# Layer 1 of a graph attention network: one row of a tile moved from TensorE to the other engines, with a pair of rows added on GpSimd

## The chip, the cores and the metric

One core of a Trainium2 chip runs the kernel. The metric is the device time of one execution in microseconds. Of the kernel before there are ten runs, and one more execution was taken by the profiler. The engines are called TensorE (PE; its weight loads PEld), VectorE (DVE), ScalarE (ACT), GpSimd (POOL) and SyncE (SP, here only a DMA queue).

## The reference

Two layers of graph attention over 10,000 nodes and 170,000 edges (80,000 random pairs in both directions, and a loop at every node), then a norm. Cut to what matters:

```python
def gat_conv(x, edge_index, W, a_src, a_dst, bias, heads, out_ch, concat):
    xl = (x @ W).reshape(n, heads, out_ch)
    alpha_src = jnp.einsum('nhc,hc->nh', xl, a_src)
    alpha_dst = jnp.einsum('nhc,hc->nh', xl, a_dst)
    e = leaky_relu(alpha_src[src] + alpha_dst[dst], 0.2)
    e = exp(e - segment_max(e, dst)[dst])
    alpha = e / (segment_sum(e, dst)[dst] + 1e-16)
    msg = xl[src] * alpha[:, :, None]
    return segment_sum(msg, dst) + bias           # concat or mean over heads

h  = gat_conv(x, edge_index, W1, ..., 4 heads, 256)   # layer 1
h1 = relu(layer_norm(h, g1, be1)) + (x @ Wr1 + br1)
h  = gat_conv(h1, edge_index, W2, ..., 1 head, 768)   # layer 2
h  = layer_norm(h, g2, be2) + (h1 @ Wr2 + br2)
out = layernorm(x + h)
```

## The kernel before

The kernel runs in three phases. The first computes the table of all nodes, `table1`: a row holds 1024 features (4 heads of 256) and its attention numbers. Beside it, it sorts the nodes by their number of edges into 79 tiles of 128 nodes. Layer 1 then takes one tile after the other, and layer 2 does the same on `table2`, with another division of the work.

The nodes of a tile lie in the 128 partitions. A tile has as many *rows* (`SLOTS[t]`) as its nodes have edges at most: row k holds, for each of the 128 nodes, the table row of its k-th neighbour, 1033 numbers. The rows are fetched by an indirect DMA that GpSimd issues (`gather`, L426) into a ring of 29 rows (`RING1`); a row's place is fetched anew when the row has been used (`ring.fetch` at the end of each k). Tiles of 14 to 17 rows are 29 of the 79: 6 of 14, 8 of 15, 7 of 16 and 8 of 17. They stand in two groups, tiles 7 to 21 and 58 to 71. None of them is cut into parts (`cuts_of` does that from 22 rows on).

For a tile of n rows the work in layer 1 is:

- The softmax of its weights `e` (`logits` and `normalised`, L489 to L514): VectorE, with one exponent on ScalarE (L497). It is the first step of the generator `weights_of(t)`.
- A weighted sum over its rows, in `acc` (PSUM). Each row is done in one of three ways. The first `on_pe(t)` rows go to TensorE: ScalarE builds four diagonal matrices from the weights (L725), TensorE multiplies them with the row (L731). Of the others, every `SHARE`-th, counted from the first, VectorE multiplies and adds by itself (`weigh`, L531, four instructions, one for each head). The rest are *shared*: ScalarE multiplies the row in place (`multiply`, L520, four instructions), VectorE adds it to `acc` (L527, one instruction).
- A norm of the sum (L542 to L558, with two small steps on ScalarE, L546 and L547), the residual (L856), a transposition, the products with `wr1` (L173) and with `w2` (L879) on TensorE, and the stores.

The kernel sets the order of each engine's instructions by hand (`manual_schedule`), so an instruction that waits holds up all that is behind it on its engine. In the loop over k, ScalarE is kept `LEAD` = 3 rows ahead (`multiplied(k + 1 + LEAD)`). The next tile's softmax is put between the last rows: `weights_of(t + 1)` takes its first step at k = n - 3 and its second, with the diagonals and TensorE's rows, at k = n - 2. The third step, with the rows beyond two for TensorE, comes at the start of the next tile, just after VectorE's statistics and the two steps L546 and L547. After row `first + 2`, GpSimd also issues the gather of the next tile's `x` rows (`xt`), and after `first` and `first + 1` the two halves of `hT` are copied by ScalarE (L698).

The rule for TensorE's rows is `min(max(SLOTS[t] // 2 - 5, 1), ON_PE1, SLOTS[t])`: 2 rows of 14 or 15, 3 of 16 or 17.

Of the kernel before, what the change touches and what calls it, by code (L numbers as in the profile page):

```python
# [48 lines left out]
LEAD = 3  # L49
DIAGONALS = 5  # L50
ON_PE2 = 512
SHARE = 4
ON_PE1 = 4
PARTED2 = 26
PARTED = 22


def chunk_counts(n_edges):
# [23 lines left out]
def gnn_kernel(ctx, tc, x, x_cols, src, dst, src_col, dst_col, W1, a_src1, a_dst1, b1, g1, be1, Wr1, br1,  # L82
               W2, a_src2, a_dst2, b2, g2, be2, Wr2, br2, out, n_edges):
    nc = tc.nc
# [3 lines left out]
    C1, C2 = H1 * DH1, H2 * DH2  # L88
# [3 lines left out]
    NT = -(-N // P)  # L92
# [4 lines left out]
    SLOTS = CAPS  # L97
# [3 lines left out]
    FIRST, TOTAL = [0] * NT, 0  # L101
# [414 lines left out]
    def multiply(row, e, dh):  # L516

        for h in range(e.shape[1]):
            s = slice(h * dh, (h + 1) * dh)
            nc.scalar.activation(row[:, s], row[:, s], AF.Copy, scale=e[:, h:h + 1])  # L520
# [122 lines left out]
    SLOTS, FIRST = [SLOTS[t] for t in TURNS], [FIRST[t] for t in TURNS]  # L643
# [4 lines left out]
    def begin_layer2(mem):  # L648


        rest = mem.shape[1]

        def at_end(n):
            nonlocal rest
            rest -= n
            return mem[:, rest:rest + n]

        firsts = [(at_end(C1), at_end(D0)) for _ in range(min(2, NT))]
        for t, (hT, xt) in enumerate(firsts):
            nc.sync.dma_start(hT, h1_d[turns[t]])  # L660
            nc.sync.dma_start(xt, x_d[turns[t]])
        wr2 = wr1.rearrange("p k n -> p (k n)")[:, :K1 * C2].rearrange("p (k n) -> p k n", n=C2)
        load(wr2, Wr2)
        br, ones = at_end(C2), at_end(P)
        yield
        nc.vector.memset(ones, 1.0)
        nc.vector.tensor_scalar(br, wr2[:, 0, :], br1_c[:, 0:1], None, op0=OP.mult)
        for k in range(1, K1):
            nc.vector.scalar_tensor_tensor(br, wr2[:, k, :], br1_c[:, k:k + 1], br, op0=OP.mult, op1=OP.add)
        yield wr2, firsts, br, ones, rest  # L670
# [4 lines left out]
    def ordered_layer1(mem):  # L675
        nc.scalar.add_instruction(mybir.InstLoadActFuncSet(name=nc.get_next_instruction_name(), act_func_set_id=6, engine=nc.scalar.engine))
        with tc.tile_pool(name="b1", bufs=1) as pool, tc.tile_pool(name="small1", bufs=2) as small, \
# [3 lines left out]
            ring = Ring(table1, RING1, {}, [mem.rearrange("p (k n) -> p k n", n=R1)])  # L681
# [30 lines left out]
            def on_pe(t):  # L712


                return min(max(SLOTS[t] // 2 - 5, 1), ON_PE1, SLOTS[t])

            def later_on_pe(t):

                return min(max((SLOTS[t] - 20) // 2, 1), ON_PE1)
# [61 lines left out]
            def cuts_of(t):  # L781

                n = SLOTS[t]
                groups = 1 if n < PARTED else -(-2 * n // ring.size)
                size = 8 if groups == 2 else (n - 5) // groups
                return [0] + [n - size * g for g in range(groups - 1, -1, -1)]

            def by_vector(t, k):
                lo = max(c for c in cuts_of(t)[:-1] if c <= k)
                return k - lo >= (later_on_pe(t) if lo else on_pe(t))  # L790

            def shared(t, k):
                return by_vector(t, k) and (k - on_pe(t)) % SHARE > 0

            last = None
            full = None
            ready = []
            ahead = iter(())
# [17 lines left out]
            for t in range(NT + 1):  # L816
                live, events = t < NT, []
                n = SLOTS[t] if live else 0
                first = done = on_pe(t) if live else 0
                cuts = cuts_of(t) if live else []  # L820
                if live and not ready:
                    ahead = weights_of(t)
                    ready += itertools.islice(ahead, 2)

                def row_of(k):
                    lo = max(c for c in es if c <= k)
                    return es[lo][0][:, k - lo], es[lo][1] if k == lo else None

                def multiplied(upto):
                    nonlocal done  # L830
                    while done < min(upto, n):
                        if shared(t, done):
                            multiply(ring.slot(FIRST[t] + done), row_of(done)[0], DH1)
                        done += 1

                if not live:
                    begin = begin_layer2(mem)
                    next(begin)
                later = iter(())
                if live:  # L840
                    es, acc = ready
                    es, later = dict(es), ahead
                if last:
                    r_before, means = last
                    stats = deviation(small, pieces(means[:, :C1], BANK))
                next(later, None)
                if full is not None:
                    store(t - 2)
                moves = []
                if live and t:  # L850
                    xT, moves = from_x(t)
                multiplied(first + 2)
                if last:
                    h = pool.tile([P, C1], F32, name="h")
                    scaled(h, [means[:, :C1]], stats, g1_b, be1_b)
                    nc.vector.scalar_tensor_tensor(h, h, 0.0, r_before[:, :C1], op0=OP.max, op1=OP.add)  # L856
                if not live:
                    begun = next(begin)
                for move in moves:
                    move()  # L860
                multiplied(first + LEAD)
                if last:
                    hT = pool.tile([P, K1, P], F32, name="hT")
                    events = [(first + j, move) for j, move in enumerate(halves(hT, h))]
                def by_wr1():
                    nonlocal r
                    if live and t:
                        r = product(xT, wr1, C1, ps_r)

                by_wr1()  # L870

                def to_layer2():
                    nonlocal full
                    nc.sync.dma_start(h1_d[t - 1], hT.rearrange("p k n -> p (k n)"))
                    full = []
                    for c in range(0, R2, BANK):
                        q = ps_half.tile([P, BANK], F32, name="half")[:, :min(BANK, R2 - c)]
                        for j in range(K1):
                            nc.tensor.matmul(q, hT[:, j, :], w2[:, j, c:c + q.shape[1]],  # L879
                                             start=(j == 0), stop=(j == K1 - 1))  # L880
                        full.append((c, q))

                if last:
                    events.append((cuts[1] - 2 * LEAD if len(cuts) > 2 else first + 2, to_layer2))

                def next_x():
                    nonlocal xt
                    xt = fetch_x(t + 1)

                if t and t + 1 < NT:  # L890
                    events.append((first + 2, next_x))
                events.sort(key=lambda event: event[0])

                def due(k):
                    while events and events[0][0] <= k:
                        events.pop(0)[1]()

                ready = []
                ahead = iter(())
                if live and t + 1 < NT:  # L900
                    ahead = weights_of(t + 1)
                for k in range(n):
                    if k + 2 * LEAD + 2 in cuts[1:-1]:
                        next(later)
                    if k + 2 * LEAD in cuts[1:-1]:
                        lo, es_lo = next(later)
                        es[lo] = es_lo
                    multiplied(k + 1 + LEAD)
                    if n - LEAD <= k < n - LEAD + 2:
                        ready += itertools.islice(ahead, 1)  # L910
                    if k + 2 in cuts[1:-1]:
                        next(later)
                    weights, fade = row_of(k)
                    if fade is not None:
                        for h in range(H1):
                            s = slice(h * DH1, (h + 1) * DH1)
                            nc.vector.scalar_tensor_tensor(acc[:, s], acc[:, s], fade[:, h:h + 1], ring.slot(FIRST[t] + k)[:, s],
                                                           op0=OP.mult, op1=OP.add)
                    if by_vector(t, k):
                        weigh(acc, ring.slot(FIRST[t] + k), weights, DH1, shared=shared(t, k))  # L920
                    ring.fetch(FIRST[t] + k + 1 + ring.size)
                    due(k)
                due(DEGREES)
                ready += itertools.islice(ahead, max(2 - len(ready), 0))
                last = None
                if live:
                    last = r, acc
# [459 lines left out]
```

## Time and profile before

| what | us |
|---|---|
| median of ten runs | 5180.73 (5172.89 to 5183.17) |
| the profiled execution | 5187.01 |
| its span, first to last instruction | 5185.2 |
| granted TensorE clock, mean | 0.964 |

Over the whole span TensorE is busy for 4766.1 us (92%), VectorE for 4281.9 (83%), GpSimd for 3301.4 (64%), ScalarE for 2818.0 (54%). The stages differ, though. Busy time in each, with the two stretches that hold the tiles of 14 to 17 rows apart:

| stretch, us from the start | what | long | PE | DVE | ACT | POOL | clock | DMA | GB/s |
|---|---|---|---|---|---|---|---|---|---|
| 0 to 907 | the table, the sorting | 907.00 | 857.65 | 482.01 | 357.95 | 436.39 | 0.98 | 0.40 | 111 |
| 1082.8 to 1500.5 | layer 1, tiles 7 to 21 | 417.70 | 405.05 | 387.22 | 317.43 | 264.13 | 1.00 | 0.96 | 353 |
| 1500.5 to 2776.8 | layer 1, longer tiles | 1276.30 | 1152.18 | 1148.73 | 1024.89 | 845.53 | 0.96 | 0.96 | 355 |
| 2776.8 to 3165.4 | layer 1, tiles 58 to 71 | 388.60 | 371.55 | 360.96 | 294.06 | 246.85 | 1.00 | 0.97 | 353 |
| 3333 to 5185 | layer 2 | 1852.00 | 1663.74 | 1597.84 | 590.26 | 1340.88 | 0.94 | 0.95 | 351 |

"DMA" is the mean busy share of the 16 DMA engines. A line of a timeline in this document reads: start, duration, engine, line of the kernel, operation, output<-input, shapes, how many instructions were merged, and in brackets how long the engine was idle ahead of them and what ended it.

### The profile page before, as it was taken

To read this page: it belongs to the slowest core of one execution; us is meant where nothing else is said; L and a number is where in the kernel's file an instruction comes from. 1 tells how busy PE (TensorE), PEld (TensorE's weight loads), DVE (VectorE), ACT (ScalarE), POOL (GpSimd) and SP (SyncE) were. 2 spreads that over 40 slices of the span, in tenths; PEclk is the share of its full clock that TensorE was granted. 3 is DMA by queue.
4 is the path that set the end of the run, shared out by engine and by line. 5 is a ranking of instruction groups with operands and counts; after the bars stand their busy time and mean duration, and the time that the engine had idled before them with its cause. 6 is when DMAs were issued, how large, how long until landed. Compare 5 with 4: busy or idle time off the path is not lost. (4 is left out here: it accounts for less than half of the span.)

```text
span 5185.2 us, 60341 instructions
## 1 busy us (share of the span) xinstructions
PE 4766.1 (92%) x15307; PEld 2864.5 (55%) x15307; DVE 4281.9 (83%) x7678; ACT 2818.0 (54%) x8248; POOL 3301.4 (64%) x3429
## 2 busy tenths in 40 slices
PE   8999998899999988788999999999999999888875
PEld 3444443455555555555555555556666666665654
DVE  4785243899999888889999999789999888888887
ACT  3443443677778887887888777433333333333232
POOL 2445455656666666666666665277777777777774
PEclk9999999899999999999999999999999999999987
DMA  4333533999999999899999999599999999999996
GB/s 160 124 102 85 90 93 126 348 336 352 358 371 370 364 350 353 297 348 351 370 371 367 359 346 337 187 384 357 367 378 376 371 365 364 362 358 357 353 350 219
DMA packets 474312, 1591.43 MB, mean 307 GB/s; under 512 B 118327, under 2 KB 122487, under 8 KB 473958
## 3 DMA queue, kind: packets, MB, share of 16 engines
q0 software_dynamic: 322384, 1286.62, 67.6%
q1 hardware_dynamic: 149520, 297.43, 16.7%
q10 hardware_dynamic: 2054, 3.42, 0.2%
q8 instruction: 129, 2.11, 0.2%
q14 instruction: 225, 1.84, 0.1%
HBM read 1431.80 MB, written 177.29 MB: 310 GB/s over the span
## 5 line engine op out<-in xcount | busy, mean ns | idle before, releaser
L426 POOL DMA_INDIRECT ring<-table,slots x2675 | 2661.6, 995 | 1281.3 <-issue 311.0
L531 DVE SCALAR_TENSOR_TENSOR acc<-ring,e,acc 128x256 f32<-128x256 f32 (+1 forms) x2546 | 1586.5, 623 | 122.2 <-PE acc L731 47.0
L520 ACT ACTIVATE ring<-ring,e 128x256 f32<-128x256 f32 x3232 | 1320.6, 508 | 0.0
L527 DVE TENSOR_TENSOR acc<-acc,ring 128x1024 f32<-128x1024 f32 x808 | 994.9, 1231 | 72.7 <-ACT ring L520 5.1
L173 PE MATMUL big<-w,xT 128*128 128x512 f32 x1896 | 825.6, 597 | 23.6 <-DMA w<-in_W_dram 10.2
L879 PE MATMUL half<-w,hT 128*128 128x512 f32 (+1 forms) x2528 | 830.4, 486 | 0.0
L173 PE MATMUL big<-wr,xT 128*128 128x512 f32 x1896 | 829.8, 594 | 0.2 <-ACT xT L698 0.2
L1033 PE MATMUL big<-wr,w 128*128 128x512 f32 (+1 forms) x2464 | 819.7, 486 | 0.0
L988 PE MATMUL big<-ring,diagonals 128*128 128x256 f32 x2754 | 679.8, 409 | 135.3 <-ACT diagonals L987 113.5
L988 PEld LDWEIGHTS big<-ring,diagonals 128*128 128x128 f32 x2754 | 559.2, 206 | 253.5 <-ACT diagonals L987 154.0
L879 PEld LDWEIGHTS half<-w,hT 128*128 128x128 f32 x2528 | 477.7, 189 | 367.7 <-issue 309.3
L1033 PEld LDWEIGHTS big<-wr,w 128*128 128x128 f32 x2464 | 468.1, 190 | 326.6 <-issue 294.8
L731 PE MATMUL acc<-ring,diagonals 128*128 128x256 f32 x2056 | 511.7, 406 | 127.7 <-ACT diagonals L725 120.0
L173 PEld LDWEIGHTS big<-w,xT 128*128 128x128 f32 x1896 | 361.7, 191 | 483.1 <-issue 462.7
L173 PEld LDWEIGHTS big<-wr,xT 128*128 128x128 f32 x1896 | 355.4, 191 | 418.0 <-issue 417.4
L731 PEld LDWEIGHTS acc<-ring,diagonals 128*128 128x128 f32 x2056 | 413.1, 204 | 222.5 <-ACT diagonals L725 148.7
L987 ACT ACTIVATE diagonals<-ident,e 128x128 f32<-128x128 f32 x1377 | 411.4, 387 | 154.3 <-DVE e L511 124.5
L546 ACT ACTIVATE sd<-mv,eps 128x1 f32<-128x1 f32 x237 | 69.5, 293 | 751.4 <-DVE mv L544 751.2
L630 DVE TENSOR_TENSOR scr<-big,ad_b 128x1024 f32<-128x1024 f32 x79 | 96.7, 1224 | 377.0 <-ACT row L627 377.0
L725 ACT ACTIVATE diagonals<-ident,e 128x128 f32<-128x128 f32 x1028 | 315.2, 388 | 166.6 <-DVE e L511 145.3
L635 POOL TENSOR_TENSOR row<-row,none 128x1024 f32<-128x1024 f32 x79 | 187.3, 2371 | 262.8 <-ACT row L627 262.3
L497 ACT ACTIVATE e<-e 128x32 f32<-128x32 f32 (+26 forms) x174 | 41.1, 236 | 552.5 <-DVE e L496 526.5
(185 smaller groups left out, 3651.2 us busy)
## 6 DMA issues: line engine op xcount, KB each, us to landing
ring<-table,slots POOLq DMA_INDIRECT x2675, 7.0
table<-row SPq DMA_DIRECT2D x79, 516.0 KB, 3.5
h_d<-hT SPq DMA_DIRECT2D x79, 512.0 KB, 6.8
w<-h_d SPq DMA_DIRECT2D x77, 512.0 KB, 8.4
table<-row SPq DMA_DIRECT2D x79, 385.0 KB, 6.1
ring<-table SPq DMA_DIRECT2D x79, 385.0 KB, 6.4
xT<-in_x_cols_dram SPq DMA_DIRECT2D x79, 384.0 KB, 4.5
x_d<-xt SPq DMA_DIRECT2D x79, 384.0 KB, 6.7
```

Of the source, the lines that this page charges most:

```text
L173: nc.tensor.matmul(p[:, c:e], aT[:, j, :], w[:, j, c:e], start=(j == 0), stop=(j == k - 1))
L426: nc.gpsimd.indirect_dma_start(out=to, out_offset=None, in_=table, in_offset=bass.IndirectOffsetOnAxis(ap=index, axis=0), **more)
L520: nc.scalar.activation(row[:, s], row[:, s], AF.Copy, scale=e[:, h:h + 1])
L527: nc.vector.tensor_add(acc[:, :c], acc[:, :c], row[:, :c])
L531: nc.vector.scalar_tensor_tensor(acc[:, s], row[:, s], e[:, h:h + 1], (acc if first is None else first)[:, s], op0=OP.mult, op1=OP.add)
L635: nc.gpsimd.tensor_add(row[:, :C1], row[:, :C1], b1_b)
L725: nc.scalar.activation(diagonals[:, k * H1 + i, :], ident, AF.Copy, scale=e[:, k, i:i + 1])
L731: nc.tensor.matmul(acc[:, c:d], diagonals[:, k * H1 + i, :], ring.slot(q + k)[:, c:d], start=(k == 0 and c % BANK == 0), stop=(k == m - 1 ...
L879: nc.tensor.matmul(q, hT[:, j, :], w2[:, j, c:c + q.shape[1]], start=(j == 0), stop=(j == K1 - 1))
L987: nc.scalar.activation(diagonals[:, (k - lo) % G, :], ident, AF.Copy, scale=e[:, k - lo, :])
L988: nc.tensor.matmul(to, diagonals[:, (k - lo) % G, :], ring.slot(at + k)[:, ON_PE2:C2], start=False, stop=(k == n - 1), skip_group_check=True)
L1033: nc.tensor.matmul(r[:, c:d], hT[:, j, :], wr2[:, j, c:d], start=False, stop=(j == K1 - 1 and d < C2), skip_group_check=True)
```

## The change

In tiles of 14 to 17 rows of layer 1, and there alone:

- TensorE takes one row fewer: 1 of 14 or 15, 2 of 16 or 17.
- Of the other rows VectorE does every fifth by itself, not every fourth. ScalarE multiplies the rest.
- GpSimd adds the eighth of these rows (number 7, counted from 0) to the ninth (number 8), after ScalarE has multiplied both; VectorE leaves out number 7 and adds number 8 alone.
- Where the next tile too has 14 to 17 rows, the first two steps of `weights_of(t + 1)` stand at k = n - 4 and n - 3, and ahead of `multiplied(k + 1 + LEAD)`, not behind it.

```diff
+PAIRED = 14, 17
...
             def on_pe(t):
-                return min(max(SLOTS[t] // 2 - 5, 1), ON_PE1, SLOTS[t])
+                return min(max(SLOTS[t] // 2 - 5 - paired(t), 1), ON_PE1, SLOTS[t])
+
+            def paired(t):
+
+                return t < NT and PAIRED[0] <= SLOTS[t] <= PAIRED[1]
...
             def shared(t, k):
-                return by_vector(t, k) and (k - on_pe(t)) % SHARE > 0
+                return by_vector(t, k) and (k - on_pe(t)) % (SHARE + paired(t)) > 0
...
+                    early = paired(t) and paired(t + 1)
+                    if early and n - LEAD - 1 <= k < n - LEAD + 1:
+                        ready += itertools.islice(ahead, 1)
                     multiplied(k + 1 + LEAD)
-                    if n - LEAD <= k < n - LEAD + 2:
+                    if not early and n - LEAD <= k < n - LEAD + 2:
                         ready += itertools.islice(ahead, 1)
+                    if paired(t) and k == first + 5:
+                        one, two = (ring.slot(FIRST[t] + first + j)[:, :C1] for j in (7, 8))
+                        nc.gpsimd.tensor_add(two, two, one)
...
-                    if by_vector(t, k):
+                    if by_vector(t, k) and not (paired(t) and k == first + 7):
                         weigh(acc, ring.slot(FIRST[t] + k), weights, DH1, shared=shared(t, k))
```

## The prediction

> **What bounds the kernel now.** I began with the busy time by stage. The tiles of 14 to 17 rows run in two stretches of layer 1, from 1082.8 to 1500.5 us (15 tiles) and from 2776.8 to 3165.4 us (14 tiles), 806 us of the span together. Then I took one tile of 16 rows and one of 14, each from one end of the norm (L856) to the next.
>
> ```profile
> core 0: us, PE busy (x) PEld busy (x) DVE busy (x) ACT busy (x) POOL busy (x), PEclk, DMA share, GB/s
> 1300.13:1327.78 27.65, 27.19 (x94) 16.26 (x93) 25.76 (x40) 21.29 (x58) 17.26 (x20) 1.00 0.99 367
> 3113.74:3139.17 25.43, 24.97 (x83) 14.31 (x83) 23.75 (x37) 19.94 (x54) 15.13 (x17) 1.00 0.96 350
> ```
>
> Two engines are full at once. TensorE is idle for 0.46 us of 27.65. VectorE is idle for 1.89 us, but in 40 instructions: 47 ns each, the step from one to the next and no wait. ScalarE has 6.4 us to spare and GpSimd 10.4. So relief of TensorE alone brings no more than VectorE gives up too, and a new wait on VectorE lengthens the tile by its whole size. When such a wait could arise is told by the order of time inside the tile, so next I read the timelines of ScalarE, VectorE and GpSimd in that 16-row tile.
>
> ```profile
> 1297.28 0.29 ACT L546 ACTIVATE sd<-mv,eps 128x1 f32<-128x1 f32 x1 [2.31 <-DVE mv L544]
> 1297.61 0.20 ACT L547 ACTIVATE sd<-sd 128x1 f32<-128x1 f32 x1
> 1297.72 1.26 ACT L725 ACTIVATE diagonals<-ident,e 128x128 f32<-128x128 f32 x4
> 1298.88 0.83 ACT L805 COPY row<-half 128x512 f32<-128x512 f32 x2
> 1299.62 1.71 ACT L520 ACTIVATE ring<-ring,e 128x256 f32<-128x256 f32 x4
> 1301.48 0.86 ACT L698 COPY xT<-half 128x512 f32<-128x512 f32 x2 [0.15 <-PE half L697]
> 1302.22 3.31 ACT L520 ACTIVATE ring<-ring,e 128x256 f32<-128x256 f32 x8
> 1305.43 1.05 ACT L698 COPY hT<-half 128x512 f32<-128x512 f32 x2
> 1306.37 9.69 ACT L520 ACTIVATE ring<-ring,e 128x256 f32<-128x256 f32 x24
> ```
>
> ScalarE waits for VectorE's mean and variance (L546) and then works without a gap through the multiplied rows. It is not ahead by a whole ring; it starts each tile from that wait.
>
> ```profile
> 1301.27 2.06 DVE L531 SCALAR_TENSOR_TENSOR acc<-ring,e,acc 128x256 f32<-128x256 f32 x4
> 1303.44 3.91 DVE L527 TENSOR_TENSOR acc<-acc,ring 128x1024 f32<-128x1024 f32 x3
> 1307.38 2.06 DVE L531 SCALAR_TENSOR_TENSOR acc<-ring,e,acc 128x256 f32<-128x256 f32 x4
> 1309.55 3.91 DVE L527 TENSOR_TENSOR acc<-acc,ring 128x1024 f32<-128x1024 f32 x3
> ```
>
> VectorE takes the rows that TensorE doesn't: one row on its own (L531, 4 instructions), three that ScalarE multiplied (L527, one add each), and so on. I number them v0, v1, ... A row on its own takes 2.17 us to the next start (1301.27 to 1303.44), a shared one 1.31 (3.94/3). Four products of ScalarE take 1.60 (1302.22 to 1305.43 is two rows). ScalarE finishes v7 at 1306.37 + 3 x 1.60 + 0.10 = 1311.27, and VectorE adds it at 1309.55 + 2 x 1.337 = 1312.22: 0.95 us of lead, the smallest in the tile.
>
> ```profile
> 1307.57 0.97 POOL L426 DMA_INDIRECT xt<-in_x_dram,order x1 [0.30 <-DVE acc L527]
> 1308.85 0.99 POOL L426 DMA_INDIRECT ring<-table,slots  x1 [0.30 <-issue]
> 1310.14 0.99 POOL L426 DMA_INDIRECT ring<-table,slots  x1 [0.30 <-issue]
> 1311.44 0.99 POOL L426 DMA_INDIRECT ring<-table,slots  x1 [0.31 <-issue]
> ```
>
> GpSimd issues one gather per row, 1.30 us apart, and just here is behind the rows.
>
> **The change, part by part.** Counts for the 6, 8, 7 and 8 tiles of 14, 15, 16 and 17 rows come from the code; zero of the clock below is VectorE's start on v0 (1301.27).
>
> *TensorE* loses one row in each of 29 tiles: 8 of the 24 matmuls that take 5.35 us in this tile (its timeline, L731), 1.78 us. That frees TensorE to 1.8 + 0.46 us of slack; on the path it is worth only VectorE's waits for it, 2.7 us over all 29 tiles (idle time before L531, released by L731: 2.1 us in the first stretch, 0.6 in the second).
>
> *VectorE.* 15 to 17 rows: own rows fall from 4 to 3, adds rise by one (15 and 16 rows: 9 to 10; 17: 10 to 11), since the pair counts as one. 4 x 0.525 = 2.10 less 1.31 is 0.8 us saved, on the path, x23 = 18.4 us. 14 rows: own rows 3 and adds 9 both before and after, nothing saved.
>
> *ScalarE* multiplies two rows more (14 rows: one), 3.2 us, and builds four diagonals fewer, 1.17 (1297.72 to 1298.88). Its 21.29 us become some 23.3, below the tile. In tiles of 16 and 17 rows the four that go are those between L547 and L805 (14 and 15 rows have none there now), so it comes to v1 earlier. The total is covered; the order is not.
>
> *The pair.* GpSimd adds v7 into v8, and VectorE skips v7 and waits for GpSimd before it adds v8. The add has the shape of phase one's L635, 128x1024 fp32 from SBUF: 79 of them took 2.347 to 2.398 us, median 2.37, while VectorE was busy beside them, and those that waited for ScalarE began 0.08 us after its copy. Now the clock. ScalarE from L546 at -3.99: L546 and L547 0.44, L805 0.74, the xT copies 0.74, the hT copies 0.94, and the seven rows v1, v2, v3, v4, v6, v7, v8 at 1.60 = 11.2; sum 14.06, with 0.1 for the last one's end: v8 is multiplied at 10.2. GpSimd has issued v4's gather by 1311.13, that is 9.86, so it is just free; the add runs 10.25 to 12.62, and VectorE can start v8 at 12.7. VectorE comes there at 2.17 + 4 x 1.31 + 2.17 + 1.31 = 10.9. It stands for **1.8 us**, and behind it in its queue are v9 and up, the next tile's softmax, the statistics, L546 and so the next tile's ScalarE start: the wait comes back in each tile and nothing catches it up. It doesn't depend on the row count, because v0 to v8 are alike in all 29.
>
> Bounds of the wait: were the add as quick as VectorE's own (L527, 1.23), it would be 0.7. If ScalarE gains nothing from the diagonals that go (the xT copies still wait for TensorE as now), v8 is 1.3 us later and the wait is 3.1. A full gather (0.99) ahead of the add would make it 2.8. I take 1.8, as the shape is L635's and TensorE's slack ends the xT wait.
>
> The Trainium skill, "GPSIMD Engine Reference", section 2.1 "Instruction dispatch", says that the first call of freshly loaded code on GpSimd costs some 6 us without an instruction in the profile. By that, should gathers and adds displace one another, the 29 adds would cost 29 x 6 = 174 us more; the trace speaks against it, as phase one's adds stand between gathers and of the 262.8 us idle before all 79 of them 262.3 are ScalarE's copy.
>
> *GpSimd's queue.* Queued behind the add is v5's gather, issued at about 12.8 instead of 10.2, 2.6 us late; at 1.30 us each the gathers catch up near the tile's end (v13's at about 24.5, two of TensorE's rows by 27, the next tile's v0 at 31). They fetch rows for the tile after next. The last row that the next softmax needs is asked for at k = S(t)+S(t+1)-30, at most 4, so at v2, ahead of the add; it lands 7.3 us after its issue (median of the DMA view in the first stretch), near 12.4, and the softmax starts after 15. Cost nothing; without that cover each us late is one more wait for VectorE (L489).
>
> *Softmax one row sooner*: rows are counted from the tile's start and VectorE begins one row sooner, so it stands ahead of the same v row as now (v10 for 16 rows). ScalarE's exponent is put ahead of the last multiplied row, needed about 4 us later. Nothing.
>
> **Sum.** 29 x 1.8 = 52.2; less 18.4; less 2.7: +31 us. That is against the profiled execution (span 5185.2, 5187.0 with what lies around it, 6.3 above the median of the ten runs); put on the median 5180.7 it gives **5212 us**. Break-even is a wait of (18.4 + 2.7)/29 = 0.73 us a tile.
>
> **Rivals.**
> *TensorE is the bound and the add is in time* (faster). For it: TensorE's 0.46 us of idle time, and all of the pair lies on engines with room. It decides where the add begins before 8.5 (10.9 less 2.4), so ScalarE would have to finish v8 1.7 us sooner than its own cadence gives; it starts from VectorE's L544 and has no idle time to lose. Then -18.4 - 2.7: 5160.
> *The wait only eats the saving* (no change): a wait of 0.4 to 1.1 us, as by the lower bound. 5180. It needs a faster add or a faster ScalarE than any row shows.
> *GpSimd falls behind for good* (slower still): if the 2.6 us are not caught up and the softmax waits for its rows, that is up to 29 x 2.6 = 75 us more, 5287. Against it: 10.4 us of GpSimd's idle time in the tile, and its 0.3 us steps show it keeps up once rows take 1.31 or more. The loading of code above would be slower by more, 5386.
>
> **How the numbers follow.** Forecast 0.80 (waits of 1.2 to 3.1: 5194 to 5250), slower still 0.07 (the loading of code 0.01 of it), no change 0.07, faster 0.06. A measurement tells 0.2% here, 10 us, from no change: slower 0.87, same 0.07, faster 0.06. Range 5186 to 5250: it leaves out most of the small cases on each side.
>
> **What would show it.** Right: in the tiles of 14 to 17 rows VectorE idle ahead of one L527-type add per tile (v8), released by GpSimd, 29 times, 1.8 us each; the new GpSimd add at 2.37 us, starting within 0.1 us of ScalarE's eighth-row products; 16-row tiles of some 28.7 us, 14-row tiles of 27.2; TensorE idle 2 us and more in each; other stages unchanged. Wrong: no such wait, or tiles shorter than now (TensorE or VectorE was the only bound), or VectorE waiting for DMA ahead of the softmax (GpSimd's lateness), or TensorE still without idle time.

## The result and the profile after

The changed kernel takes 5210.93 us in the median of 8 runs (5203.46 to 5218.51). The kernel before takes 5180.15 us (median of 28 runs, those beside the changed kernel included). The ratio is 1.006, 95% interval 1.0052 to 1.0069: 0.6% slower, 31 us. The forecast was 5212.

The profiled execution of the changed kernel has a span of 5204.7 us, 19.5 more than before's. Its two stretches with the tiles of 14 to 17 rows now run from 1082.5 to 1515.7 and from 2786.3 to 3190.0 us: 433.2 and 403.7 us, together 836.9 against 806.2 (taken from one L856, now L861, to the other). That is +30.7, the whole of the difference between the medians. The longer tiles between them took 1270.6 us instead of 1276.3 and layer 2 some 5 us less in that one execution, where no instruction was changed; why, is open. From here on the sum of the two stretches is used beside the ratio.

Line numbers after the change: the products of ScalarE are L521, VectorE's add L528, its own rows L532, the softmax's first instruction L490, TensorE's rows L736, the copies of xT and hT L699. GpSimd's new add is L921.

The same windows as before, one tile of 16 rows and one of 14:

```profile
core 0: us, PE busy (x) PEld busy (x) DVE busy (x) ACT busy (x) POOL busy (x), PEclk, DMA share, GB/s
1336.83:1365.55 28.72, 26.05 (x86) 15.02 (x86) 25.19 (x38) 23.20 (x63) 20.25 (x23) 1.00 0.97 352
3135.43:3162.60 27.17, 24.32 (x78) 13.50 (x78) 23.74 (x36) 20.44 (x55) 18.54 (x19) 1.00 0.94 335
```

The tile of 16 rows grew from 27.65 to 28.72 us, the one of 14 rows from 25.43 to 27.17, though TensorE is busy for 1.1 and 0.65 us less and VectorE for 0.6 us less and the same. TensorE's idle time rose from 0.46 to 2.67 us, and VectorE's from 1.89 to 3.53 in the tile of 16. Both engines that were full now stand, so a wait has come in. The timelines of VectorE and GpSimd in that 16-row tile:

```profile
1345.42 2.06 DVE L532 SCALAR_TENSOR_TENSOR acc<-ring,e,acc 128x256 f32<-128x256 f32 x4
1347.59 1.23 DVE L528 TENSOR_TENSOR acc<-acc,ring 128x1024 f32<-128x1024 f32 x1
1350.61 2.57 DVE L528 TENSOR_TENSOR acc<-acc,ring 128x1024 f32<-128x1024 f32 x2 [1.79 <-POOL ring L921]
```
```profile
1346.84 0.99 POOL L427 DMA_INDIRECT ring<-table,slots  x1 [0.30 <-issue]
...
1348.21 2.36 POOL L921 TENSOR_TENSOR ring<-ring 128x1024 f32<-128x1024 f32 x1 [0.39 <-ACT ring L521]
1350.72 1.00 POOL L427 DMA_INDIRECT ring<-table,slots  x1
```

VectorE has added v6 by 1348.82 and begins v8 at 1350.61: 1.79 us idle, and the releaser is GpSimd's add, which itself waited for ScalarE until 1348.21. VectorE's start on v0 is 1337.97 in this tile, so the add begins at 10.24 on the prediction's clock (worked out there as 10.25) and VectorE goes on at 12.64 (12.7). All 29 adds together, from the profile's view of line 921: the three numbers behind x29 are the shortest, the median and the longest in ns; behind a releaser or a waiting line stand the total us and the number of times.

```profile
L921 POOL TENSOR_TENSOR ring<-ring x29: 2353/2362/2377, 1093.9 to 3174.0; 128x1024 f32<-128x1024 f32 x29
...
ACT ring L521: 9.7, 25
who waited for it (us, times):
DVE acc L528: 53.2, 29
```

53.2 us in 29 tiles is 1.83 us each.

One thing changed that the forecast had not named, the granted clock of TensorE. Over the two stretches it was 1.00 before and is 0.96 after:

```profile
1082.50:1515.70 433.20, 393.65 (x1245) 225.66 (x1246) 378.81 (x564) 342.80 (x899) 298.13 (x312) 0.96 0.94 339
2786.30:3190.00 403.70, 363.16 (x1140) 206.20 (x1140) 353.64 (x528) 317.16 (x827) 275.28 (x290) 0.96 0.95 339
```

In 14 places the trace shows a granted clock of 0.5 for 3.4 or 6.8 us, 61 us together; a product of L174 took 1061 ns there and 592 elsewhere (medians). TensorE's busy time in the stretches fell by 19.8 us (776.6 to 756.8), not by 29 x 1.78 = 51.6; half of the 61 us is about the difference. It cost no time here, because TensorE was idle for at least 1.37 us in every one of the 29 tiles.

### The profile page after: what moved, and what is told of

Its sections match the earlier page's. It is cut to its first block, busy times and chain, and to the rows that moved or that the text cites. A ratio compares the mean times of both kernels' runs of the same rounds, so it can differ in the third digit from the quotient of the medians.

```text
span 5204.7 us, 59923 instructions
## 1 busy us (share of the span) xinstructions
PE 4739.4 (91%) x15075; PEld 2831.5 (54%) x15075; DVE 4264.8 (82%) x7609; ACT 2865.8 (55%) x8340; POOL 3355.5 (64%) x3458
## 5 line engine op out<-in xcount | busy, mean ns | idle before, releaser
L532 DVE SCALAR_TENSOR_TENSOR acc<-ring,e,acc 128x512 f32<-128x512 f32 (+1 forms) x2454 | 1541.3, 628 | 114.1 <-PE acc L736 42.9
L521 ACT ACTIVATE ring<-ring,e 128x256 f32<-128x256 f32 x3440 | 1409.8, 509 | 0.0
L528 DVE TENSOR_TENSOR acc<-acc,ring 128x1024 f32<-128x1024 f32 x831 | 1023.4, 1232 | 124.3 <-POOL ring L921 53.2
L174 PE MATMUL big<-w,xT 128*128 128x512 f32 x1896 | 825.4, 597 | 23.8 <-DMA w<-in_W_dram 10.5
L174 PE MATMUL big<-wr,xT 128*128 128x512 f32 x1896 | 845.0, 603 | 0.2 <-ACT xT L699 0.2
L174 PEld LDWEIGHTS big<-w,xT 128*128 128x128 f32 x1896 | 361.7, 191 | 483.3 <-issue 462.8
L174 PEld LDWEIGHTS big<-wr,xT 128*128 128x128 f32 x1896 | 362.5, 195 | 427.3 <-issue 426.7
L736 PE MATMUL acc<-ring,diagonals 128*128 128x256 f32 x1824 | 458.3, 408 | 121.5 <-ACT diagonals L730 109.1
L998 ACT ACTIVATE diagonals<-ident,e 128x128 f32<-128x128 f32 x1377 | 412.3, 387 | 162.5 <-DVE e L512 128.1
L736 PEld LDWEIGHTS acc<-ring,diagonals 128*128 128x128 f32 x1824 | 368.5, 205 | 207.7 <-ACT diagonals L730 134.2
L730 ACT ACTIVATE diagonals<-ident,e 128x128 f32<-128x128 f32 x912 | 279.9, 388 | 136.8 <-DVE e L512 116.3
```

The lines of the kernel that those rows point to most:

```text
L174: nc.tensor.matmul(p[:, c:e], aT[:, j, :], w[:, j, c:e], start=(j == 0), stop=(j == k - 1))
L528: nc.vector.tensor_add(acc[:, :c], acc[:, :c], row[:, :c])
L532: nc.vector.scalar_tensor_tensor(acc[:, s], row[:, s], e[:, h:h + 1], (acc if first is None else first)[:, s], op0=OP.mult, op1=OP.add)
L730: nc.scalar.activation(diagonals[:, k * H1 + i, :], ident, AF.Copy, scale=e[:, k, i:i + 1])
L736: nc.tensor.matmul(acc[:, c:d], diagonals[:, k * H1 + i, :], ring.slot(q + k)[:, c:d], start=(k == 0 and c % BANK == 0), stop=(k == m - 1 ...
L998: nc.scalar.activation(diagonals[:, (k - lo) % G, :], ident, AF.Copy, scale=e[:, k - lo, :])
```

## The experiments

Ten more runs were profiled in three groups, each group with the kernel before timed on the same chip. On the chip of the first two groups layer 2 took longer, whatever the kernel: the profile of b0_before has a span of 5518.7 us, with 301 GB/s in layer 2 where the first profile has 351, but 806.8 us in the two stretches. So each ratio is against the kernel before on the same chip, and the stretches can be compared across all.

| run | ratio (95%) | two stretches, us | tiles of 14, 15, 16, 17 rows, median us |
|---|---|---|---|
| before, first profile | | 806.2 | 25.89, 27.70, 27.80, 29.18 |
| b0_before | | 806.8 | 25.89, 27.71, 27.80, 29.18 |
| changed, first profile | 1.006 (1.0052 to 1.0069) | 836.9 | 27.23, 28.72, 28.75, 30.07 |
| a0_after | 1.0063 (1.0048 to 1.0078) | 839.1 | 27.46, 28.74, 28.81, 30.10 |
| e1_no_pair | 1.003 (1.0014 to 1.0047) | 823.2 | 26.90, 28.27, 28.30, 29.67 |
| e2_pair_9_11 | 1.0057 (1.0041 to 1.0072) | 835.5 | 28.26, 29.05, 29.17, 28.58 |
| e3_tensor_row_only | 1.0069 (1.005 to 1.0087) | 846.8 | 27.64, 29.09, 29.14, 30.50 |
| e4_share5_only | 0.9988 (0.9978 to 0.9998) | 798.8 | 26.08, 26.93, 27.90, 28.42 |
| e5_no_early | 1.0045 (1.0029 to 1.0061) | 837.5 | 27.41, 28.70, 28.76, 30.02 |
| e6_own_row_ahead | 0.9974 (0.9964 to 0.9985) | 795.4 | 25.50, 26.87, 28.30, 28.27 |
| e7_pair_keep_tensor | 1.0033 (1.0019 to 1.0048) | 825.3 | 26.64, 27.42, 28.64, 29.92 |
| e8_two_rows_ahead | 0.996 (0.9947 to 0.9974) | 785.8 | 25.56, 26.84, 26.92, 28.27 |

**e1_no_pair.** The changed kernel without the pair.

```diff
-                    if paired(t) and k == first + 5:
-                        one, two = (ring.slot(FIRST[t] + first + j)[:, :C1] for j in (7, 8))
-                        nc.gpsimd.tensor_add(two, two, one)
...
-                    if by_vector(t, k) and not (paired(t) and k == first + 7):
+                    if by_vector(t, k):
```

> The changed kernel without GpSimd's add: VectorE adds the eighth row by itself. Theory (VectorE stands 1.8 us a tile for the pair, which spares it one add of 1.31): per tile of 15 to 17 rows one own row less (2.10) and two adds more (2.62) than before, +0.5 x 23; per tile of 14 rows one add more, +1.3 x 6; less the 2.7 us of waits for TensorE: +17 us, 5197, so 14 us faster than the changed kernel though an engine's help is taken away. Rival (the loss comes from ScalarE's added rows or the gathers, not from the pair): the 29 adds of 1.31 come on top, 5211 + 38 = 5249.

The stretches are 823.2 us: +17.0 over before, as the theory has it, and 13.7 less than with the pair. VectorE took back 29 adds and the kernel became faster. The pair costs more than it spares.

**e3_tensor_row_only** and **e4_share5_only.** The other two edits, each alone, without the pair and with the softmax where it was. The lines are shown against the changed kernel.

```diff
 e3:
-                return by_vector(t, k) and (k - on_pe(t)) % (SHARE + paired(t)) > 0
+                return by_vector(t, k) and (k - on_pe(t)) % SHARE > 0
 e4:
-                return min(max(SLOTS[t] // 2 - 5 - paired(t), 1), ON_PE1, SLOTS[t])
+                return min(max(SLOTS[t] // 2 - 5, 1), ON_PE1, SLOTS[t])
```

> Only TensorE's row is taken away; VectorE does every fourth row by itself as before, no pair, softmax where it was. Theory (VectorE is full as well): one own row more in 14-row tiles (2.1 x 6), one add more in the others (1.31 x 23), less 2.7: +40, 5220. Rival (TensorE is what bounds these tiles): 1.78 us less in each of 29, 5128.

> Only every fifth row instead of every fourth is VectorE's own; TensorE keeps its row, no pair. Theory (TensorE and VectorE are both full): VectorE has 0.8 us less in tiles of 15 to 17 rows, but TensorE lets through only what it has idle: some 0.8 in the eight tiles of 15 rows and 0.75 in the eight of 17, nothing in 14 and 16: about -12, 5168. Rival (VectorE alone bounds): -18 and more, 5160. Rival (TensorE alone bounds): no change, 5180.

e3: +40.6 us in the stretches, where TensorE as the only bound would have given -52. e4: -7.4 us against before, and in the medians by tile size what two full engines let through: 15 rows -0.77 us, 17 rows -0.76, while 14 and 16 rows, where TensorE was idle for only 0.46 us in most tiles, gained nothing (two of the seven tiles of 16 rows did get shorter, by 0.8 and 0.9 us). The total is 5 us short of the -12 expected; two tiles of this execution (30.0 and 30.6 us, of 17 and 16 rows) hold most of that, and why they are long is open. Either edit alone is held by the other engine.

**e2_pair_9_11.** The pair is moved to where ScalarE is further ahead: row 9 is added into row 11.

```diff
-                    if paired(t) and k == first + 5:
-                        one, two = (ring.slot(FIRST[t] + first + j)[:, :C1] for j in (7, 8))
+                    if paired(t) and k == first + 8:
+                        one, two = (ring.slot(FIRST[t] + first + j)[:, :C1] for j in (9, 11))
...
-                    if by_vector(t, k) and not (paired(t) and k == first + 7):
+                    if by_vector(t, k) and not (paired(t) and k == first + 9):
```

> The changed kernel with another pair: GpSimd adds row 9 into row 11, issued three rows later. Theory (the place of the pair costs, not GpSimd's work): ScalarE has row 11 multiplied at 13.4 on the tile's clock, the add runs to 15.9, VectorE comes to row 11 at 16.4 after the softmax and row 10: no wait, VectorE's saving of 0.8 x 23 and 2.7 us stays, 5159, faster than before by 0.4%. Rival (the add costs GpSimd's queue or the gathers, wherever it stands): 5200 or more, with VectorE waiting for DMA or for GpSimd.

The wait for the add was gone (0.2 us in all) and the lost time was still there: 835.5 us. The expectation failed. The rival's size came true, but not the waits that it named: VectorE waited for no DMA in these tiles. It is *busy* where it had waited. The softmax's first instruction in a tile of 16 rows before, then the timelines of VectorE and GpSimd in the same tile of this run:

```profile
1289.00 0.29 DVE L489 TENSOR_TENSOR e<-ring 128x24 f32<-128x24 f32 x2
```
```profile
1305.76 3.91 DVE L528 TENSOR_TENSOR acc<-acc,ring 128x1024 f32<-128x1024 f32 x3
1309.58 2.41 DVE L490 TENSOR_TENSOR e<-ring 128x24 f32<-128x24 f32 x2
1312.02 0.23 DVE L191 SCALAR_TENSOR_TENSOR e<-e 128x64 f32<-128x64 f32 x1
```
```profile
1308.90 0.99 POOL L427 DMA_INDIRECT ring<-table,slots  x1 [0.30 <-issue]
1309.91 2.01 POOL L921 TENSOR_TENSOR ring<-ring 128x1024 f32<-128x1024 f32 x1
```

L490 adds two small operands, both in SBUF; before (as L489) it took 0.29 us in this tile, as two instructions, and 0.22 where it is one. Here it takes 2.41 and ends just behind GpSimd's add (1311.92). In each of the 21 tiles of 14 to 16 rows one small softmax instruction with two operands in SBUF was drawn out in this way, until 0.03 to 0.09 us behind the add's end: L490 in ten tiles, L191 in nine, L497 in two, 48 us together. In tiles of 17 rows the softmax stands behind row 10: there VectorE's own row 10 (L532, one operand in PSUM and one in SBUF) ran beside the add at its usual 0.49 us each, and L490 met only the end of the add in six of the eight (it took 0.3 to 0.75 us; 1.55 in the first of these tiles, and in one the two did not meet). Those are the fast tiles: 28.58 us, 0.6 less than before. The Trainium skill, "GPSIMD Engine Reference", states that GpSimd's interfaces to SBUF are shared with VectorE, with contention against VectorE instructions that have two SBUF inputs (sections 1 "Specifications" and 8 "Key points"). The trace agrees and adds the size: such an instruction ends only when the add is over, which made 0.2 to 0.3 us into as much as 2.7. The add itself lasts 2.0 us; the two longest of these instructions (2.66 and 2.68 us) began 0.6 us ahead of its recorded start, and what held them there is open.

**e5_no_early.** The softmax back at k = n - 3.

```diff
-                    early = paired(t) and paired(t + 1)
+                    early = False
```

> The changed kernel with the softmax at its old place, k = n - 3 and behind the multiplication. Theory (the softmax's place costs and brings nothing): as the changed kernel, 0.6% slower than before, the two stretches 837 us together. Rival (it hides TensorE's start): 1 us or more a tile on top, 866 us.

837.5 us: the place of the softmax brings and costs nothing, with the wait there. (The ratio is lower than the changed kernel's 1.006. On that chip 31 us of 5520 are 0.56%, which lies inside the interval.)

**e7_pair_keep_tensor.** TensorE keeps its row, so in tiles of 16 and 17 rows ScalarE still builds four diagonals ahead of the multiplied rows. The edit is that of e4 in `on_pe` with `early = False`, the pair left in.

> The changed kernel with TensorE's row kept as before (2 of 14 and 15 rows, 3 of 16 and 17) and the softmax at its old place. Theory (ScalarE's order sets the wait): in tiles of 16 and 17 rows the four diagonals stand ahead of the multiplied rows again, 1.17 us, so VectorE waits 3.0 us there and 1.8 in tiles of 14 and 15; with its work 1.31 less in 14-row tiles and 2.1 in the others that is 6 x 0.5 - 8 x 0.3 + 15 x 0.9 = +14 us, 820 us in the two stretches. Rival (GpSimd's queue sets the wait): 1.8 in all of them, -4 us, 802.

The waits for the add, with total us, times and the longest:

```profile
DVE acc L528 <- POOL ring L921: 74.2, 29, 3.3
```

By tile the median wait is 2.98 us with 16 rows and 2.97 with 17, 1.80 with 15: what the diagonals' 1.17 us add to 1.8. With 14 rows it is 2.43, 0.6 more than expected; there TensorE is full again and ScalarE waits for its transposes of x in some of these tiles (1.29 us in the first). Where the diagonals come back, the wait grows by them: ScalarE's order sets it, not GpSimd's queue. The stretches are 825.3 us against 820 expected and 802 by the rival.

**e6_own_row_ahead.** The pair stays 7 and 8; VectorE does row 10, one of its own, before row 8. The gathers into the places of rows 8 to 10 go out together after row 9.

```diff
-                    weights, fade = row_of(k)
+                    at = first + {8: 10, 9: 8, 10: 9}.get(k - first, k - first) if paired(t) else k
+                    weights, fade = row_of(at)
...
-                    if by_vector(t, k) and not (paired(t) and k == first + 7):
-                        weigh(acc, ring.slot(FIRST[t] + k), weights, DH1, shared=shared(t, k))
-                    ring.fetch(FIRST[t] + k + 1 + ring.size)
+                    if by_vector(t, at) and not (paired(t) and k == first + 7):
+                        weigh(acc, ring.slot(FIRST[t] + at), weights, DH1, shared=shared(t, at))
+                    if not (paired(t) and first + 8 <= k < first + 10):
+                        ring.fetch(FIRST[t] + k + 1 + ring.size)
```

> The kernel before, for a profile on the same chip as the others of this group. Tiles of 14 to 17 rows as in the first profile: 25.9, 27.7, 27.8 and 29.2 us, 806 us in all.

b0_before: 806.8 us, and the four sizes within 0.02 us of the first profile.

> The changed kernel, but VectorE does row 10, one of its own that needs neither ScalarE nor GpSimd, between row 6 and row 8, so that GpSimd's add runs beside it; then 8, 9, 11. Theory (the loss is VectorE's wait for the add, and an add beside VectorE's own row hinders nothing): VectorE comes to row 8 at 13.0 on the tile's clock, the add ends at 12.6; no wait, and the softmax starts after it. The saving of 18.4 and 2.7 us stays: the two stretches 785 us against 806, 0.4% faster than before. Rival (GpSimd's add hinders VectorE also in its own rows, or its delayed gathers come late): 1 us and more a tile is lost again, 814 us and up.

795.4 us and 0.26% faster than before: most of the loss is gone, and 10 us of the expected gain are missing. In the medians of the tiles of 15 and 17 rows all of it is there (26.87 and 28.27). VectorE still waited for the add in 12 tiles, 7.6 us together, most in those of 16 rows, where ScalarE's copy of xT came 1.1 to 3.4 us late in five of the seven and with it the whole row of products. The granted clock goes with a part of this: in eight of the 29 tiles it was 0.5 for 3.4 us, and in the tile after each of these the copy was 0.3 to 2.0 us behind its usual place; seven of the 12 waits, 4.6 of the 7.6 us, follow so. No run isolates it, and the latest copy (3.4 us) has no such stretch in the tile ahead of it.

**e8_two_rows_ahead** and **a0_after.** Row 9 too goes ahead of row 8, 1.3 us more room for the add.

```diff
-                    at = first + {8: 10, 9: 8, 10: 9}.get(k - first, k - first) if paired(t) else k
+                    at = first + {8: 10, 9: 9, 10: 8}.get(k - first, k - first) if paired(t) else k
```

> As e6_own_row_ahead, but VectorE does row 9 as well before row 8: order 6, 10, 9, 8. In e6 VectorE still waited 7.6 us in 12 tiles, where ScalarE's copies of xT came late. Theory: VectorE now comes to row 8 at 14.3, the add ends at 12.6, or 14.4 where it is late: no wait for GpSimd, the two stretches some 788 us against 806, 0.35% faster than before. Rival (the late adds now meet the softmax, whose first instruction reads two operands from SBUF and stood still beside GpSimd's add in e2): L490 takes 1 us and more in those tiles, and nothing is won over e6, 795.

> The changed kernel once more, on the chip of this group. Theory: the two stretches 837 us, the wait 1.8 us in each of 29 tiles, 0.6% slower than before or, where layer 2 takes longer, the same 30 us on a longer time.

a0_after: 839.1 us, median waits of 1.80 to 1.86 us in the four sizes, 1.0063. e8: 785.8 us in the stretches, 20.4 less than before, and 5155.97 us (median of 5) against 5175.21 on that chip: faster than both. This run was on a chip whose layer 2 took its usual time, so part of the step from e6 may be the chip's. In one tile of 14 rows the softmax still met the add, as the rival has it: L490 took 1.07 us. A 16-row tile of e8: its window (columns as above), VectorE and GpSimd.

```profile
1321.30:1348.30 27.00, 26.01 (x90) 15.26 (x88) 25.19 (x39) 23.37 (x62) 20.83 (x23) 1.00 1.01 377
```
```profile
1332.08 1.23 DVE L528 TENSOR_TENSOR acc<-acc,ring 128x1024 f32<-128x1024 f32 x1
1333.35 2.07 DVE L532 SCALAR_TENSOR_TENSOR acc<-ring,e,acc 128x256 f32<-128x256 f32 x4
1335.52 1.23 DVE L528 TENSOR_TENSOR acc<-acc,ring 128x1024 f32<-128x1024 f32 x1
1336.66 0.28 DVE L490 TENSOR_TENSOR e<-ring 128x12 f32<-128x12 f32 x2
```
```profile
1333.00 2.37 POOL L921 TENSOR_TENSOR ring<-ring 128x1024 f32<-128x1024 f32 x1 [0.56 <-ACT ring L521]
```

VectorE's work is the same 25.19 us as in the changed kernel's tile, and the add the same 2.37, but it lies beside VectorE's own row 10 (2.07 us, not drawn out) and is over before the softmax. In none of the 29 tiles does VectorE stand idle for it.

## Why the prediction was right, point by point

- *The wait at v8*, 1.8 us in each of 29 tiles, 52.2 in all: measured 1.83 and 53.2. The clock that gave it held at each mark: add from 10.24 (10.25), 2.36 us long (2.37 by phase one's row), VectorE on at 12.64 (12.7). The wait does not depend on the row count: the medians are 1.79 to 1.81 in all four sizes.
- *ScalarE's order sets it.* Shown by e7, with the diagonals put back: 2.98 us in tiles of 16 and 17 rows. GpSimd's queue is little of it: in 25 of 29 tiles the add waited for ScalarE. In the other four it followed a gather without a gap, and two of these have the longest waits, 2.17 and 2.61 us.
- *VectorE's saving*, 18.4 us: its busy time fell by 17.1 (4281.9 to 4264.8). e8, where the wait is away, shows the saving and the 2.7 us of TensorE as time: -20.4 us where the prediction has -21.1.
- *TensorE alone is worth little.* Shown by e3 (+40.6 us). The 1.78 us that the row was to free in each tile did not come in full: the busy time fell by 19.8 us over the 29 tiles, with the granted clock at 0.96 (1.00 before). The sum did not use the 1.78, so the forecast did not suffer. e4 shows that VectorE alone is worth as little where TensorE has nothing idle.
- *GpSimd's later gathers cost nothing*: ahead of the softmax VectorE waited for no gather in the first stretch of the changed kernel, and once, for 0.5 us, in the second.
- *The softmax's place costs nothing*: e5, 837.5 against 836.9 us.
- *The loading of code*, the risk that the prediction took from the Trainium skill, "GPSIMD Engine Reference", section 2.1: no add shows it. GpSimd's idle time ahead of all 29 adds is 9.7 us, and all of it is ended by ScalarE.
- The sum of +31 us was +30.7 in the stretches and +31 in the medians. The wait was 1.0 us more than forecast, the rest of the sum 1.4 us more in the other direction.
- What the prediction did not look at is what GpSimd's add does to VectorE's instructions with two operands in SBUF. It did not matter where the pair stood, since VectorE was waiting or adding from PSUM; it decided e2.

## What to carry to other kernels

Where two engines are full at once, relief of one is worth what the other gives up, and work handed to an idle engine is free only if its result is ready when the full engine comes to it: set the clock of both from the wait that starts them, not from their idle totals. If it is late, put work that doesn't need it in between; here the same instructions in another order made 0.6% slower into 0.4% faster. An add on GpSimd should lie beside VectorE instructions that read PSUM, not beside small ones with two operands in SBUF.

## What the runs showed of the hardware that was not expected

- A VectorE instruction with two SBUF operands (L490, L191 or L497; 0.2 to 0.3 us by itself) took up to 2.7 us beside GpSimd's 128x1024 add (e2) and ended with it. A reduction with one SBUF operand (L494) kept its 0.27 us in the one tile of e2 where it ran beside the add, and VectorE's 128x256 multiply-adds with one operand in PSUM kept their 0.49 us (e8: 2.07 for four).
- GpSimd's add took 2.00 to 2.02 us in 28 of e2's 29 tiles, where its operands lie two rows of the ring apart, and 2.354 in the one where the ring's end puts them 27 rows apart. With neighbouring rows, or 28 apart at the ring's end, it took 2.35 to 2.38 in every tile of the changed kernel and of e8, whether VectorE was waiting or busy. Why the distance should matter is open.
- The granted clock of TensorE fell to 0.5 for 3.4 or 6.8 us at a time once TensorE had lost its row: 14 to 17 times in the 29 tiles of the changed kernel (two profiles), e1, e2, e3 and e5, 8 times in e6, 6 in e8. Where TensorE kept the row, it was never or once (before 0, b0 1, e4 0, e7 1). So a part of the relief of TensorE was lost again; what the clock goes by, these runs don't show.
